# A two-layer graph attention kernel: where the first inputs of layer 2 lie, and when br1's product is made

## The chip, the cores and the metric

The kernel runs on one core of a Trainium2 chip. The metric is the time of the whole program on the device in microseconds (us), median of several runs. A core has five engines with a queue each: TensorE (PE in the profile; its weight loads are PEld), VectorE (DVE), ScalarE (ACT), GpSimd (POOL) and SyncE (SP). SP does no arithmetic here: it issues DMA transfers. POOL issues the indirect DMAs, which gather or scatter rows by a list of row numbers. Both kinds of transfer run on the core's 16 DMA engines. [...] an instruction that waits holds up everything behind it in its queue.

## The reference

There are 10000 nodes with 768 features and 170000 edges (80000 drawn, their reverses, and a loop at each node), sorted by target. Cut to what matters:

```python
def gat_conv(x, edge_index, W, a_src, a_dst, bias, heads, out_ch, concat):
    xl = (x @ W).reshape(n, heads, out_ch)
    e = leaky_relu(alpha_src[src] + alpha_dst[dst], 0.2)
    e = exp(e - segment_max(e, dst)[dst])
    alpha = e / (segment_sum(e, dst)[dst] + 1e-16)
    return segment_sum(xl[src] * alpha, dst) + bias

h1 = relu(layer_norm(gat_conv(x, W1, 4 heads of 256), g1, be1)) + (x @ Wr1 + br1)
h2 = layer_norm(gat_conv(h1, W2, 1 head of 768), g2, be2) + (h1 @ Wr2 + br2)
out = plain_layer_norm(x + h2)
```

All of it is float32. The kernel never adds br1 to h1: it carries h1 - br1. What br1 contributes behind it is a row that is the same for every node: br1 @ W2 for layer 2's attention, br1 @ Wr2 for its residual.

## The kernel before, in words

**Stages.** The first stage makes table 1 (x @ W1 and its attention logits for each node) and sorts the nodes by degree. Then 79 tiles of 128 nodes are worked through twice, by `ordered_layer1` and by `ordered_layer2`. A tile's nodes have about the same degree, so a tile is `SLOTS[t]` gathers of 128 table rows, one row for each node: 8, 10, 11, 12, 12, 13 slots for the first tiles, up to 41 in the middle, and down to 9 at the end. Layer 1 writes each tile's product h1 @ W2 to table 2 in DRAM (`table2`), its transposed h1 to `h1_d` and its x to `x_d`. Layer 2 gathers rows of all tiles from table 2, so its gathers begin once layer 1's last row of tiles has landed.

**Layer 2, for each tile t.** The first slot holds the tile's own rows and comes by SP (L452); the others are gathered by POOL (L424). VectorE makes the logits e from the last columns of the slots (L477 to L499). The 768 columns are then weighted and summed over the slots: the first 512 by VectorE into `acc` (`weigh`, L519), the last 256 by TensorE, which multiplies each slot with a diagonal matrix of its weights (diagonals by ScalarE at L891, products at L892, bias at L887). TensorE also makes the residual r = x + h1 @ Wr2 in PSUM (`residual`, L903 for x, L906 for h1). After the last slot VectorE takes the statistics of the sum (L561, in `norms`), normalises with g2 and be2, adds r, takes statistics again, and ScalarE and an indirect DMA of POOL (L925) write the rows out.

**Buffers.** The ring holds `RING2` = 38 slots of 770 floats a partition. Slot q of all tiles, counted through, lies at q modulo 38. `ring.fetch(upto)` issues the loads of all slots below `upto`; a gather into a used slot waits until VectorE and TensorE have read it. The ring belongs to pool `b2`, which lies where layer 1's pool `b1` lay: the first instruction that uses `b2` on an engine waits until all work on `b1` is done. `wr2` takes the place of `wr1`, outside these pools, and is loaded earlier. The transposed h1 and the x of a tile come by SP into `parts` (`fetch_x`, L867 and L868), pieces of the memory of W2, two for each kind in turn; `ins` holds those that are on their way.

**Constants.** `spread` loads a vector to all 128 partitions (L143). At the start of layer 2, b2, g2, be2, br2 and `shift` (br1 @ W2) are spread; `be2_b` gets br2 (L860), `b2_b` gets the shift (L861). br1 is copied along the free axis into `brT` (L585), and the product brT @ wr2 (L952, recorded at the helper's line L171) gives br1 @ Wr2 in all partitions; it is added to `be2_b` at L973, ahead of the first tile's statistics.

**Order.** Inside a stage the order is written out by hand: each engine executes its instructions in the order of the program. In tile t's loop over its slots, VectorE also makes the logits of tile t + 1 (at slot `turn`) and the norm of tile t - 1 (at slots 3, 6 and 9), between the sums. SP's order at the start of layer 2 is: Wr2; b2, g2, be2; br2, shift; the own row of tile 0; h and x of tile 0; h and x of tile 1; then own rows of tiles 1, 2, 3 inside the ring (`ring.fetch(RING2)`, L931). TensorE's order is residual(0); tile 0's weights; br1's product; residual(1); tile 1's weights; residual(2). GpSimd issues 7 gathers for tile 0 (L859) and then the 27 others that the ring holds, 34 in all, before slots are used again.

Of the kernel before, what the change touches and what calls it, by code (L numbers as in the profile page):

```python
# [35 lines left out]
P = 128  # L36
# [11 lines left out]
RING2 = 38  # L48
# [31 lines left out]
def gnn_kernel(ctx, tc, x, x_cols, src, dst, src_col, dst_col, W1, a_src1, a_dst1, b1, g1, be1, Wr1, br1,  # L80
               W2, a_src2, a_dst2, b2, g2, be2, Wr2, br2, out, n_edges):
    nc = tc.nc
    N, D0 = out.shape
# [6 lines left out]
    NT = -(-N // P)  # L90
# [48 lines left out]
    def spread(pool, v, name, queue=None):  # L139

        n = v.shape[-1] if len(v.shape) == 1 else v.shape[0] * v.shape[1]
        b = pool.tile([P, n], F32, name=name)
        (queue or nc.scalar).dma_start(b, bass.AP(tensor=v.tensor, offset=v.offset, ap=[[0, P], [1, n]]))  # L143
        return b
# [437 lines left out]
    def spread_br1(pool, name):  # L582

        to = pool.tile([P, K1, P], F32, name=name)
        nc.vector.tensor_copy(to, br1_c[:, :, None].to_broadcast([P, K1, P]))  # L585
        return to
# [259 lines left out]
    def ordered_layer2():  # L846
        nonlocal ps_big
        with tc.tile_pool(name="b2", bufs=1) as pool, tc.tile_pool(name="small2", bufs=2) as small, \
                tc.tile_pool(name="ps_acc2", bufs=2, space=PSUM) as ps_acc, \
                tc.tile_pool(name="ps_q2", bufs=3, space=PSUM) as ps_big, tc.manual_schedule():  # L850

            wr2 = wr1.rearrange("p k n -> p (k n)")[:, :K1 * C2].rearrange("p (k n) -> p k n", n=C2)
            load(wr2, Wr2)
            parts = pieces(w2.rearrange("p k n -> p (k n)")[:, :6 * C1], C1)
            b2_b, g2_b, be2_b = (spread(pool, v, n, nc.sync)
                                 for v, n in ((b2, "b2"), (g2, "g2"), (be2, "be2")))
            adds = [spread(pool, br2, "out", nc.sync), spread(pool, shift, "brT", nc.sync)]
            ring = Ring(pool, table2, R2, RING2, dict(zip(FIRST, TURNS)))
            ring.fetch(SLOTS[0])  # L859
            nc.vector.tensor_add(be2_b, be2_b, adds[0])  # L860
            nc.vector.tensor_add(b2_b, b2_b, adds[1][:, :C2])  # L861
            brT = spread_br1(pool, "brT")

            def fetch_x(t):

                hT, xt = parts[t % 2], parts[2 + t % 2][:, :D0]
                nc.sync.dma_start(hT, h1_d[t])  # L867
                nc.sync.dma_start(xt, x_d[t])  # L868
                return hT.rearrange("p (k n) -> p k n", n=P), xt

            ones = pool.tile([1, P], F32, name="ones")
            nc.vector.memset(ones, 1.0)

            def whole(t):
                return SLOTS[t] <= ring.size

            def weights_of(t):


                n = SLOTS[t]  # L880
                ad = small.tile([P, H2], F32, name="ad")
                nc.vector.tensor_add(ad, ring.slot(FIRST[t])[:, C2:C2 + H2], lift)
                e, _ = logits(small, ring, FIRST[t], FIRST[t] + n, ad, H2, C2)
                yield e
                normalised(small, e, H2, t)
                to = rs[t][:, C2:2 * C2 - ON_PE2]
                nc.tensor.matmul(to, ones, b2_b[0:1, ON_PE2:], start=False, stop=False, skip_group_check=True)  # L887
                for k in range(n):
                    if k % G == 0:
                        diagonals = pool.tile([P, G, P], F32, name="diagonals", bufs=DIAGONALS)  # L890
                    nc.scalar.activation(diagonals[:, k % G, :], ident, AF.Copy, scale=e[:, k, :])  # L891
                    nc.tensor.matmul(to, diagonals[:, k % G, :], ring.slot(FIRST[t] + k)[:, ON_PE2:C2],  # L892
                                     start=False, stop=(k == n - 1), skip_group_check=True)
                yield

            def residual(t):


                hT, xt = ins.pop(t)
                r = ps_big.tile([P, 2 * BANK], F32, name="big")  # L900
                for c in range(0, C2, BANK):
                    d = min(C2, c + BANK)
                    nc.tensor.matmul(r[:, c:d], ident, xt[:, c:d], start=True, stop=False,  # L903
                                     skip_group_check=True)
                    for j in range(K1):
                        nc.tensor.matmul(r[:, c:d], hT[:, j, :], wr2[:, j, c:d], start=False,  # L906
                                         stop=(j == K1 - 1 and (d < C2 or not whole(t))),
                                         skip_group_check=True)
                return r

            def norms(t, h, r, means):

                stats = deviation(small, [a for m in means for a in pieces(m, C2 - ON_PE2)])
                yield
                scaled(h, means, stats, g2_b, be2_b)
                nc.vector.tensor_add(h, h, r[:, :C2])
                mean, inv = deviation(small, pieces(h, C2 // 2))
                yield
                nc.vector.reciprocal(inv, inv)
                less = small.tile([P, 1], F32, name="less")  # L920
                nc.vector.scalar_tensor_tensor(less, mean, -1.0, inv, op0=OP.mult, op1=OP.mult)
                o = pool.tile([P, C2], F32, name="out")
                nc.scalar.activation(o, h, AF.Identity, bias=less, scale=inv)
                yield
                nc.gpsimd.indirect_dma_start(  # L925
                    out=out, out_offset=bass.IndirectOffsetOnAxis(ap=nodes(t), axis=0),
                    in_=o, in_offset=None, bounds_check=N - 1, oob_is_err=False)

            assert C2 % BANK and C2 % BANK + C2 - ON_PE2 <= BANK
            ins = {t: fetch_x(t) for t in range(min(2, NT))}  # L930
            ring.fetch(RING2)  # L931
            rs = {0: residual(0)}
            last = iter(())
            ready = []
            assert whole(0) and NT > 1
            for t in range(NT):
                n = SLOTS[t]
                if 0 < t < NT - 1:
                    rs[t + 1] = residual(t + 1)
                h = parts[4 + t % 2][:, :C2]  # L940
                if not whole(t):
                    for _ in last:
                        pass
                    ad = small.tile([P, H2], F32, name="ad")
                    nc.vector.tensor_add(ad, ring.slot(FIRST[t])[:, C2:C2 + H2], lift)
                    attend_parts(small, ring, h, h, ad, b2_b, H2, DH2, t)
                    last = norms(t, h, rs[t], [h])
                else:
                    e = (ready or list(weights_of(t)))[0]
                    acc = ps_acc.tile([P, BANK], F32, name="acc")  # L950
                    if not t:
                        q = product(brT, wr2, C2)  # L952
                        rs[1] = residual(1)
                    next(last, None)
                    ready, ahead, turn = [], iter(()), n
                    if t + 1 < NT and SLOTS[t + 1] + LEAD <= ring.size:

                        ahead = weights_of(t + 1)
                        turn = min(max(n // 3, n + SLOTS[t + 1] + 2 * LEAD - ring.size), n - LEAD)
                    for k in range(n):  # L960
                        if k in (turn, turn + LEAD):
                            ready += itertools.islice(ahead, 1)
                        if k in (LEAD, 2 * LEAD, 3 * LEAD):
                            next(last, None)
                        weigh(acc, ring.slot(FIRST[t] + k), e[:, k], ON_PE2, None if k else b2_b)
                        ring.fetch(FIRST[t] + k + 1 + ring.size)
                        if t + 2 < NT and k == n // 2:
                            ins[t + 2] = fetch_x(t + 2)
                    ready += ahead
                    for _ in last:  # L970
                        pass
                    if not t:
                        nc.vector.tensor_add(be2_b, be2_b, q[:, :C2])  # L973
                    last = norms(t, h, rs[t], [acc, rs[t][:, C2:2 * C2 - ON_PE2]])
                if t + 2 < NT and t + 2 not in ins:
                    ins[t + 2] = fetch_x(t + 2)
            for _ in last:
                pass
# [270 lines left out]
```

## Time and profile before

| What | us |
|---|---|
| median of 3 runs | 5388.15 (5386.93 to 5388.26) |
| the profiled execution | 5386.19 |
| its span, first to last instruction | 5384.3 |
| busy in the span: PE / DVE / ACT / POOL | 4721.3 / 4348.2 / 3138.9 / 3238.2 |
| layer 1's last row of table 2 issued by SP | 3433.48 |
| layer 2's first gather on POOL | 3437.43 |
| TensorE's first product of layer 2 | 3461.82 |
| last instruction, the last rows out on POOL | 5372.45 |

Times in the profile count from the start of the span. A row of the timeline is: start, length in us, engine, line and operation, output and inputs with partitions x elements, how many, and in brackets how long the engine stood idle before it and what released it. "SPq" and "POOLq" are the queues' own instructions. The tile names are cut at their first digit, so that `w` stands for W2's memory (parts) and `wr` for Wr1's (wr2), `big` for any of TensorE's results. A row of windows gives each engine's busy time in a stretch, then the granted clock of TensorE as a share of full speed, the busy share of the DMA engines and what they moved in GB/s. The slices of the page are fortieths of the span, 134.6 us each, with the busy share in tenths; layer 2 fills slices 25 to 39. The ends of products are modelled, so a busy TensorE isn't one at its peak.

### The profile page before, as it was taken

Reading aid. Unit: us, or ns where it says so; the run is one execution under the profiler, and the core shown is the slowest. Engines: PE = TensorE matmul, PEld = TensorE weight load, DVE = VectorE, ACT = ScalarE, POOL = GpSimd, SP = SyncE. Lnnn points to the kernel's source line nnn. Section 1 sums busy time; section 2 is a strip of 40 time slices with the busy share of each in tenths; the row PEclk is TensorE's granted clock in tenths of the full one; section 3 lists DMA queues with packets and bytes.
Section 4 is the critical chain, followed back from the end, with each engine's and each line's share of the span. In section 5 each row is a group of like instructions: output and inputs, shape, how many; then the busy total and the mean of one; then the engine's idle time right before and its main releaser. Section 6 shows DMA issues by size and latency. Waiting matters only on the chain. (4 is left out here: it accounts for less than half of the span.)

```text
span 5384.3 us, 59633 instructions
## 1 busy us (share of the span) xinstructions
PE 4721.3 (88%) x15011; PEld 2818.7 (52%) x15011; DVE 4348.2 (81%) x8008; ACT 3138.9 (58%) x8204; POOL 3238.2 (60%) x3159
## 2 busy tenths in 40 slices
PE   8999996999999886478999999799988846889998
PEld 3444443555555543245555555466665534556665
DVE  5784244899999888888999999499887876878998
ACT  3434343787888877778888888344433313334443
POOL 3446455455666665556666554367776766767774
PEclk9999998999999998789999999899998978989999
DMA  4333635899999996899999998699999998999995
GB/s 155 126 98 90 90 93 202 307 338 342 359 358 369 358 346 252 306 323 355 359 365 362 350 334 303 221 327 377 369 337 327 332 301 301 341 328 354 369 382 216
DMA packets 474308, 1591.37 MB, mean 296 GB/s; under 512 B 118327, under 2 KB 122487, under 8 KB 473958
## 3 DMA queue, kind: packets, MB, share of 16 engines
q0 software_dynamic: 322384, 1286.62, 66.3%
q1 hardware_dynamic: 149520, 297.43, 16.3%
q10 hardware_dynamic: 2054, 3.42, 0.2%
q8 instruction: 126, 2.06, 0.2%
q14 instruction: 224, 1.84, 0.1%
HBM read 1431.80 MB, written 177.29 MB: 299 GB/s over the span
## 5 line engine op out<-in xcount | busy, mean ns | idle before, releaser
L424 POOL DMA_INDIRECT ring<-table,slots x2675 | 2659.6, 994 | 1486.7 <-DVE acc L519 366.4
L519 DVE SCALAR_TENSOR_TENSOR acc<-ring,e,acc 128x256 f32<-128x256 f32 (+1 forms) x2538 | 1570.8, 619 | 113.3 <-PE acc L725 37.7
L508 ACT ACTIVATE ring<-ring,e 128x256 f32<-128x256 f32 x3320 | 1351.5, 507 | 0.2
L515 DVE TENSOR_TENSOR acc<-acc,ring 128x1024 f32<-128x1024 f32 x830 | 1021.3, 1230 | 80.6 <-ACT ring L508 9.2
L171 PE MATMUL big<-w,xT 128*128 128x512 f32 x1896 | 826.1, 597 | 27.0 <-DMA w<-in_W_dram 9.6
L906 PE MATMUL big<-wr,w 128*128 128x512 f32 (+1 forms) x2528 | 846.4, 488 | 0.0
L892 PE MATMUL big<-ring,diagonals 128*128 128x256 f32 x2672 | 667.2, 412 | 193.3 <-ACT diagonals L891 180.3
L171 PE MATMUL big<-wr,xT 128*128 128x512 f32 x1896 | 835.4, 597 | 0.2 <-ACT xT L688 0.2
L803 PE MATMUL half<-w,hT 128*128 128x512 f32 (+1 forms) x2528 | 830.4, 486 | 0.0
L892 PEld LDWEIGHTS big<-ring,diagonals 128*128 128x128 f32 x2672 | 548.2, 208 | 309.8 <-ACT diagonals L891 211.8
L803 PEld LDWEIGHTS half<-w,hT 128*128 128x128 f32 x2528 | 477.8, 189 | 372.7 <-issue 310.7
L906 PEld LDWEIGHTS big<-wr,w 128*128 128x128 f32 x2528 | 482.6, 191 | 340.1 <-issue 307.5
L725 PE MATMUL acc<-ring,diagonals 128*128 128x256 f32 x1816 | 452.2, 406 | 220.5 <-ACT diagonals L719 220.2
L171 PEld LDWEIGHTS big<-w,xT 128*128 128x128 f32 x1896 | 362.5, 192 | 486.5 <-issue 467.6
L171 PEld LDWEIGHTS big<-wr,xT 128*128 128x128 f32 x1896 | 357.7, 192 | 421.6 <-issue 420.9
L725 PEld LDWEIGHTS acc<-ring,diagonals 128*128 128x128 f32 x1816 | 365.9, 204 | 299.7 <-ACT diagonals L719 242.7
L891 ACT ACTIVATE diagonals<-ident,e 128x128 f32<-128x128 f32 x1336 | 400.5, 387 | 147.6 <-DVE e L499 129.3
L565 ACT ACTIVATE sd<-mv,eps 128x1 f32<-128x1 f32 x237 | 69.8, 295 | 638.0 <-DVE mv L563 637.7
L649 DVE TENSOR_TENSOR scr<-big,ad_b 128x1024 f32<-128x1024 f32 x79 | 96.7, 1224 | 381.6 <-ACT row L646 381.6
L654 POOL TENSOR_TENSOR row<-row,none 128x1024 f32<-128x1024 f32 x79 | 187.0, 2368 | 266.8 <-ACT row L646 266.3
L719 ACT ACTIVATE diagonals<-ident,e 128x128 f32<-128x128 f32 x908 | 278.5, 387 | 117.6 <-DVE e L499 117.6
L485 ACT ACT_TABLE_LOAD x153 | 196.3, 1283 | 219.7 <-DVE e L484 108.1
(172 smaller groups left out, 3813.4 us busy)
## 6 DMA issues: line engine op xcount, KB each, us to landing
ring<-table,slots POOLq DMA_INDIRECT x2675, 6.9
table<-row SPq DMA_DIRECT2D x79, 516.0 KB, 3.7
h_d<-hT SPq DMA_DIRECT2D x79, 512.0 KB, 6.9
w<-h_d SPq DMA_DIRECT2D x79, 512.0 KB, 8.3
table<-row SPq DMA_DIRECT2D x79, 385.0 KB, 6.4
ring<-table SPq DMA_DIRECT2D x79, 385.0 KB, 6.4
xT<-in_x_cols_dram SPq DMA_DIRECT2D x79, 384.0 KB, 4.5
x_d<-xt SPq DMA_DIRECT2D x79, 384.0 KB, 6.7
```

Of the source, the lines that this page charges most:

```text
L171: nc.tensor.matmul(p[:, c:e], aT[:, j, :], w[:, j, c:e], start=(j == 0), stop=(j == k - 1))
L424: nc.gpsimd.indirect_dma_start(out=to, out_offset=None, in_=table, in_offset=bass.IndirectOffsetOnAxis(ap=index, axis=0), **more)
L485: nc.scalar.activation(e, e, AF.Exp)
L508: nc.scalar.activation(row[:, s], row[:, s], AF.Copy, scale=e[:, h:h + 1])
L515: nc.vector.tensor_add(acc[:, :c], acc[:, :c], row[:, :c])
L519: nc.vector.scalar_tensor_tensor(acc[:, s], row[:, s], e[:, h:h + 1], (acc if first is None else first)[:, s], op0=OP.mult, op1=OP.add)
L719: nc.scalar.activation(diagonals[:, k * H1 + i, :], ident, AF.Copy, scale=e[:, k, i:i + 1])
L725: nc.tensor.matmul(acc[:, c:d], diagonals[:, k * H1 + i, :], ring.slot(FIRST[t] + k)[:, c:d], start=(k == 0 and c % BANK == 0), stop=(k == ...
L803: nc.tensor.matmul(q, hT[:, j, :], w2[:, j, c:c + q.shape[1]], start=(j == 0), stop=(j == K1 - 1))
L891: nc.scalar.activation(diagonals[:, k % G, :], ident, AF.Copy, scale=e[:, k, :])
L892: nc.tensor.matmul(to, diagonals[:, k % G, :], ring.slot(FIRST[t] + k)[:, ON_PE2:C2], start=False, stop=(k == n - 1), skip_group_check=True)
L906: nc.tensor.matmul(r[:, c:d], hT[:, j, :], wr2[:, j, c:d], start=False, stop=(j == K1 - 1 and (d < C2 or not whole(t))), skip_group_check= ...
```

## The change

Layer 2's first inputs leave W2's memory. The ring is made first, and its last 4608 floats a partition (slots 32 to 37, all but 12 floats of them) hold, from the end downwards: the spread br1 (1024), h and x of tile 1 (1024 and 768), h and x of tile 0. Later tiles use `parts` as before. With that:

- br1 is spread into the ring's end as VectorE's first instruction of the stage, and its product is TensorE's first, ahead of residual(0).
- SP's order becomes: Wr2; h and x of tile 0; own row of tile 0; shift; b2; h and x of tile 1; g2, be2; br2; own rows of tiles 1 to 3.
- `ring.fetch(RING2)` moves behind residual(1), since slots 32 to 37 are free only then.
- br2 is added to be2 at the end of tile 0's loop, just ahead of br1 @ Wr2, in place of the start; br2 and the shift share a buffer with `out`, so `brT` as a tile of the pool is gone.

```diff
-            b2_b, g2_b, be2_b = (spread(pool, v, n, nc.sync)
-                                 for v, n in ((b2, "b2"), (g2, "g2"), (be2, "be2")))
-            adds = [spread(pool, br2, "out", nc.sync), spread(pool, shift, "brT", nc.sync)]
             ring = Ring(pool, table2, R2, RING2, dict(zip(FIRST, TURNS)))
-            ring.fetch(SLOTS[0])
-            nc.vector.tensor_add(be2_b, be2_b, adds[0])
-            nc.vector.tensor_add(b2_b, b2_b, adds[1][:, :C2])
-            brT = spread_br1(pool, "brT")
+            rest, flat = RING2 * R2, ring.rows.rearrange("p k n -> p (k n)")
+
+            def at_end(n):
+                nonlocal rest
+                rest -= n
+                return flat[:, rest:rest + n]
+
+            brT = at_end(C1).rearrange("p (k n) -> p k n", n=P)
+            nc.vector.tensor_copy(brT, br1_c[:, :, None].to_broadcast([P, K1, P]))
+            firsts = [(at_end(C1), at_end(D0)) for _ in range(min(2, NT))][::-1]
 
             def fetch_x(t):
 
-                hT, xt = parts[t % 2], parts[2 + t % 2][:, :D0]
+                hT, xt = firsts[t] if t < 2 else (parts[t % 2], parts[2 + t % 2][:, :D0])
...
+            ins = {0: fetch_x(0)}
+            ring.fetch(SLOTS[0])
+            adds = [spread(pool, shift, "out", nc.sync)]
+            b2_b = spread(pool, b2, "b2", nc.sync)
+            ins[1] = fetch_x(1)
+            g2_b, be2_b = (spread(pool, v, n, nc.sync) for v, n in ((g2, "g2"), (be2, "be2")))
+            nc.vector.tensor_add(b2_b, b2_b, adds[0][:, :C2])
+            adds.append(spread(pool, br2, "out", nc.sync))
+            assert SLOTS[0] <= rest // R2 and NT > 1
...
-            ins = {t: fetch_x(t) for t in range(min(2, NT))}
-            ring.fetch(RING2)
+            q = product(brT, wr2, C2)
             rs = {0: residual(0)}
...
                     if not t:
-                        q = product(brT, wr2, C2)
                         rs[1] = residual(1)
+                        ring.fetch(RING2)
...
                     if not t:
+                        nc.vector.tensor_add(be2_b, be2_b, adds[1])
                         nc.vector.tensor_add(be2_b, be2_b, q[:, :C2])
```

More of the change, by code (lines that the diff above doesn't have):

```diff
@@ L934, in ordered_layer2 @@
             ready = []
-            assert whole(0) and NT > 1
+            assert whole(0)
             for t in range(NT):
```

## The prediction

> **What bounds the kernel now.** I read the slices of the page first, then the windows of 20 us around the change of layers, then the timeline there, then VectorE's waits behind it.
>
> ```profile
> span 5384.3 us, 59633 instructions
> ...
> PE   8999996999999886478999999799988846889998
> ...
> DVE  5784244899999888888999999499887876878998
> ...
> DMA  4333635899999996899999998699999998999995
> ```
>
> One notch matters here: at slice 25 the table for layer 2 has just been completed, and DVE falls to 4 and DMA to 6. The windows resolve it (columns: length, busy us of PE, weight load, DVE, ACT, POOL, then clock, DMA share, GB/s):
>
> ```profile
> 3420.00:3440.00 20.00, 12.98 (x46) 7.63 (x44) 0.00 (x0) 2.51 (x5) 1.95 (x3) 0.93 0.30 105
> 3440.00:3460.00 20.00, 0.00 (x0) 0.00 (x0) 2.90 (x5) 0.00 (x0) 11.88 (x12) 0.50 1.02 293
> 3460.00:3480.00 20.00, 18.18 (x51) 10.60 (x52) 7.66 (x26) 5.00 (x14) 12.11 (x13) 0.80 1.02 402
> 3480.00:3500.00 20.00, 20.00 (x61) 11.21 (x60) 9.69 (x21) 6.54 (x13) 13.76 (x15) 1.00 1.01 394
> 3520.00:3540.00 20.00, 20.00 (x74) 13.55 (x73) 18.44 (x40) 9.06 (x24) 12.14 (x13) 1.00 0.87 303
> ```
>
> Up to 3500 the DMA engines are full, while TensorE first has nothing and then cannot stop; at 3520 to 3540 TensorE and VectorE are full and the DMA engines are not (0.87). The timeline says why (start, us, engine, line):
>
> ```profile
> 3433.48 0.32 SPq L747 DMA_DIRECT2D table<-row  x1
> 3436.61 0.33 SPq L143 DMA_DIRECT2D b<-in_b_dram  x1
> 3440.22 0.89 SPq L868 DMA_DIRECT2D w<-x_d  x1
> 3460.21 0.17 DVE L477 TENSOR_TENSOR e<-ring,ad 128x8 f32<-128x8 f32 x1 [5.27 <-DMA ring<-table,slots]
> 3461.82 2.05 PE L903 MATMUL big<-w,ident 128*128 128x512 f32 x2 [28.78 <-DMA w<-x_d]
> 3475.19 0.17 DVE L477 TENSOR_TENSOR e<-ring,ad 128x10 f32<-128x10 f32 x1 [3.57 <-DMA ring<-table,slots]
> 3480.78 10.48 PE L171 MATMUL big<-wr,brT 128*128 128x512 f32 x32
> 3484.23 0.95 POOL L424 DMA_INDIRECT ring<-table,slots  x1 [0.30 <-issue]
> 3491.30 0.95 DVE L973 TENSOR_TENSOR be<-be,big 128x768 f32<-128x768 f32 x1 [9.93 <-PE big L171]
> 3502.80 0.69 PE L887 MATMUL big<-b,ones 1*128 1x256 f32 x2
> 3504.39 0.94 POOL L424 DMA_INDIRECT ring<-table,slots  x1 [5.71 <-DVE sd L919]
> ```
>
> TensorE waits 28.8 us for x of tile 0, which stands behind five spread vectors and an own row on SP's queue. It then does residual(0), tile 0's weights and br1's product in a row, and VectorE, through with tile 0's rows, stands 9.93 us for that product. Tile 1's slots come free late, and GpSimd's gathers stand 5.7 us (3498.7 to 3504.4). The delay is felt for a while after, as five tiles show in VectorE's waits, of 3508 to 3560 and of 3560 to 3620 (total us, times, longest):
>
> ```profile
> DVE st L561 <- PE big L892: 1.5, 2, 0.8
> DVE st L561 <- PE big L892: 1.7, 3, 0.8
> ```
>
> From 3740 on VectorE waits for gathers instead (4.3 us in 3740 to 3800, 4.6 in the next 60 us), and gathers for slots.
>
> **What the Trainium skill says.** "TensorE: Matmul & The Clock Gate", Part 1, What's actually happening: the throttled clock is the default, a window of some 3.4 us without work brings it back, and as much work releases it. The trace agrees: the last product ends at 3433.04, the clock is 0.78 in 3436 to 3438 and 0.50 until about 3467, some 5 us after TensorE begins. "DMA: Bandwidth & Descriptors", Queues, rings and completion order: each DMA engine takes packets in turn from the queues that have work. So SP's loads and GpSimd's gathers share the 16 engines, and order counts within a queue; the trace agrees, since x of tile 0 needs 21.6 us behind 2.3 MB of SP's own. "Perfetto Trace Analysis", Identifying the Most-Contended Engine: busy time of matmuls is no good measure of load; I use the period of a tile instead.
>
> **The change part by part.**
>
> Loads. SP's first load of this pool is released at 3436.61 by the last row's store; the new tiles lie in the same pool, so I let h and x of tile 0 start then and not earlier. What SP moved: two issues (0.49 and 0.89 us) go ahead of five spreads (about 0.4 us each) and the own row; h and x of tile 1 ahead of g2, be2 and br2. The bytes ahead of tile 1's own row stay 4.1 MB, so its landing (3471.5) stays. By the record of before, 1152 KB of SP's queue had landed at 3442.5, so x of tile 0 (896 KB) is there by about 3442. In before x of tile 1 landed at 3468.8; it now has 1.2 MB less ahead of it. A new wait: br2 goes into the shift's buffer, so SP stands until VectorE has added shift and b2 (2049 KB of the queue, so about 3452), and the own rows of tiles 1 to 3 stand behind it. I cost it at nothing, because SP's transfers already issued keep the engines busy to about 3465; without that cover tile 1's logits are late one for one.
>
> TensorE. The spread of br1 (0.69 us on VectorE) no longer waits for the sums of L860 and L861, so the product starts at about 3437.5; Wr2 was issued at 3410.96 and took about 10 us. It takes 10.48 us, plus the throttled start: in before the first two groups of residual(0) took 2.05 and 9.12 us against 1.02 and 7.03 of residual(2), 3.1 us more. It ends near 3451. residual(0), 11.7 us (3507.85 to 3519.55 for residual(2)), to 3462.7. Weights of tile 0 wait for the logits, whose gathers I leave at 3460.2, and diagonals at 3463.6; 4.2 us (3476.59 to 3480.78), to 3468. residual(1) to 3479.6, in place of 3502.8. Then tile 1's diagonals (3479.15 on) and 5.1 us: 3485 in place of 3507.85. residual(2) needs h and x loaded at about 3478, which took 9.6 us: start 3490, and with a throttled start of 2.6 its weights end near 3510, in place of 3525. TensorE is **15 us** ahead.
>
> VectorE. Tile 1's logits wait for the same gathers (3475.19), so tile 0's rows are done at 3481.4 as before. The 9.93 us go; the sum with br2, moved here, costs 0.95: **9.0 us** ahead. Next it wants tile 2's last gather, issued at 3477.98 and 8.5 us under way, so 3486.5, at 3495.80 - 9.0 = 3486.8: just in time. h and x of tile 3, whose buffers are now free at once, come some 20 us earlier and put 0.9 MB (2.4 us at 380 GB/s) in the way; I charge 0.5. The waits of five tiles for TensorE, 1.5 + 1.7 = **3.2 us**, go too, as TensorE leads by more.
>
> Gathers. Slots 32 to 37 now hold the first inputs, so the gathers into them wait for the product, residual(0) and residual(1), and GpSimd's queue waits behind them, with every later gather and the first store of rows out. The first that needs residual(1) is slot 34, the 31st gather, at 3484.23 in before. residual(1) ends at 3479.6: hidden by 4.6 us; without that cover it costs its delay one for one. The stalls at 3498.7, 3515.7 (4.5 us), 3534 and later go, since tiles 1 to 4 free their slots earlier; at 1.25 us a gather the queue can gain more than 12 us before 3620.
>
> Sum: 9.93 - 0.95 + 3.2 - 0.5 = **11.7 us**. After 3740 gathers, VectorE and slots wait for each other in a ring, nothing is tied to absolute time, and I let the lead pass unchanged to the end. The profiled execution took 5386.19 (span 5384.3 and 1.9 around it), so 5374.5; the median of the runs is 1.96 above it: **5376.4**.
>
> Bounds not shown in the trace: tile 0's gathers may land 3 us earlier or later, since the spreads now share time with later gathers (-3 to +3); the lead in the stage of gathers is kept between a third and, if TensorE's lead decides, the whole of 15 to 17.
>
> **Rivals.** *Partly given back* (0.20): the DMA engines, 0.87 to 0.96 busy between 3500 and 3640, have only 12.4 us of idle share, and the extra early loads and queueing eat some of it. For it: share 1.00 from 3640. Against: they moved 402 GB/s at 3460, and 370 there. Gain 3 to 9: 5379 to 5385. *TensorE's lead decides* (0.12): if gathers run 15 us ahead by 3600, VectorE's later waits for them shrink too; 5370 to 5373. *Nothing arrives* (0.06): tile 1 and 2 are limited by the full DMA engines whatever TensorE does, 5386 to 5390; against it stands the 9.93 us wait that names the product. *Slower* (0.06): gathers stand for residual(1). It decides from an end after 3484 plus the 12 us gained, so 3496; if tile 1's inputs or tile 0's logits come so late that residual(1) ends where it did, 3502.8, GpSimd stands 18.6 us and the net is +7: 5395. Against: x of tile 1 now has less ahead of it.
>
> **How the numbers follow.** My forecast, gain 10 to 14, has 0.56. The measurement can tell about 0.2% from no change, 10.8 us. Of the forecast 0.48 lies beyond that, and TensorE's 0.12: faster 0.60. The rest of the forecast, given back and nothing: about 0.33 same. Slower 0.07. The range 5370 to 5385 takes gains of 3 to 18 and leaves out the last two rivals and little more.
>
> **What would show it.** br1's product starts near 3437.5 and ends near 3451; residual(0) follows without a gap; VectorE's 9.93 us wait is gone; residual(1) ends before the gather of slot 34; the gathers no longer stand at 3498.7; the waits of L561 for TensorE are gone up to 3620, and the wait of VectorE for gathers begins about 12 us sooner. Wrong it would be if gathers wait on L906 or L171 after 3484, if the loads of h and x do not land before 3451, or if the lead at 3600 is there and the end has not moved.

## The result, and the profile after

The changed kernel takes 5374.60 us (median of 8 runs, 5369.76 to 5378.14), the kernel before beside it 5388.98 (8 runs, 5386.93 to 5391.94). The ratio is 0.9971, 95% interval 0.9961 to 0.9982: 14.4 us or 0.27% less, and 1.8 us below the forecast of 5376.4. The profiled execution of the changed kernel took 5377.65, with a span of 5375.9.

The two spans differ by only 8.4 us, because layer 1, whose code is the same in both, ended later in the second execution: SP issued its last row of table 2 at 3435.89 and not at 3433.48. So all comparisons of traces here count from that row. From there to the end it is 1950.8 us before (5384.31 - 3433.48) and 1940.0 after: 10.9 us less.

The page of the changed kernel, slices of 134.4 us:

```profile
span 5375.9 us, 59639 instructions
...
PE   8999996999999886478999999999988846889998
...
DVE  5884244899999888888999999599887786778998
```

At slice 25 PE has risen from 7 to 9 and DVE from 4 to 5. The windows of 20 us of the changed kernel show more (busy us of PE, weight load, DVE, ACT, POOL, then clock, DMA share, GB/s):

```profile
3440.00:3460.00 20.00, 19.96 (x51) 10.31 (x52) 1.10 (x3) 0.00 (x0) 12.31 (x13) 0.91 1.00 280
3480.00:3500.00 20.00, 17.17 (x57) 10.81 (x56) 17.54 (x42) 9.22 (x22) 14.75 (x15) 0.91 1.02 402
3520.00:3540.00 20.00, 20.00 (x74) 13.44 (x72) 18.50 (x41) 7.90 (x18) 15.35 (x16) 1.00 1.00 381
```

TensorE, which had nothing to do in 3440 to 3460, is full. VectorE's busy time in 3480 to 3500 went from 9.69 to 17.54. And at 3520 to 3540 GpSimd issues 16 instructions in place of 13, so that the DMA engines are full (1.00, before 0.87). The timeline of the changed kernel from layer 1's last row on (start, us, engine, line, idle time before and its releaser):

```profile
3435.89 0.32 SPq L747 DMA_DIRECT2D table<-row  x1
3440.04 12.28 PE L171 MATMUL big<-wr,ring 128*128 128x512 f32 x32 [4.59 <-DVE ring L865]
3452.16 1.02 PE L917 MATMUL big<-ring,ident 128*128 128x512 f32 x2
3463.19 0.17 DVE L477 TENSOR_TENSOR e<-ring,ad 128x8 f32<-128x8 f32 x1 [6.49 <-DMA ring<-table,slots]
3467.03 5.41 PE L906 MATMUL big<-ring,diagonals 128*128 128x256 f32 x16 [2.48 <-ACT diagonals L905]
3472.28 1.02 PE L917 MATMUL big<-ring,ident 128*128 128x512 f32 x2
3476.87 0.17 DVE L477 TENSOR_TENSOR e<-ring,ad 128x10 f32<-128x10 f32 x1 [2.83 <-DMA ring<-table,slots]
3484.01 0.95 DVE L987 TENSOR_TENSOR be<-be,big 128x768 f32<-128x768 f32 x1
3486.28 1.37 POOL L424 DMA_INDIRECT ring<-table,slots  x1 [0.30 <-PE big L906]
3490.01 0.17 DVE L477 TENSOR_TENSOR e<-ring,ad 128x11 f32<-128x11 f32 x1 [1.53 <-DMA ring<-table,slots]
```

The product runs while the loads land, and residual(0) (L917 at 3452.16) follows it without a gap. The sum with br1's product (L987) waits for nothing: the 9.93 us are gone. The gather of slot 34 (3486.28) comes after residual(1), which ended at 3483.98, and stands only its usual 0.30. What is left of VectorE's waits from 3480 to 3620 (total us, times, longest):

```profile
DVE e L477 <- DMA ring<-table,slots: 1.5, 1, 1.5
DVE sd L576 <- ACT sd L565: 0.7, 1, 0.7
```

VectorE no longer waits for TensorE at all. In the kernel before this list was 9.9 us for br1's product and 3.2 us of L561.

**Where the lead goes.** A lead here is how much earlier than in the kernel before the same step comes. The table follows one gather (the 101st of layer 2) and two additions of residuals on VectorE (those of tiles 8 and 20), each counted from layer 1's last row in its own trace. First the two rows of before, then those of after, for the gather and for tile 20:

```profile
3597.82 0.94 POOL L424 DMA_INDIRECT ring<-table,slots  x1 [0.30 <-issue]
3889.06 0.95 DVE L916 TENSOR_TENSOR w<-w,big 128x768 f32<-128x768 f32 x1
```

```profile
3583.55 0.95 POOL L424 DMA_INDIRECT ring<-table,slots  x1 [0.30 <-DVE acc L519]
3875.12 0.95 DVE L930 TENSOR_TENSOR w<-w,big 128x768 f32<-128x768 f32 x1
```

The gather: 3597.82 - 3433.48 = 164.34 against 3583.55 - 3435.89 = 147.66, a lead of 16.7. Tile 20: 455.58 against 439.23, a lead of 16.3. In the same way for the kernels of the experiments below:

| kernel | gather 101 | VectorE, tile 8 | VectorE, tile 20 | end of the span |
|---|---|---|---|---|
| product first, loads as before | 10.5 | 10.5 | 12.7 | 11.8 |
| loads first, product as before | 11.3 | 6.6 | 13.5 | 15.4 |
| the change | 16.7 | 11.1 | 16.3 | 10.9 |
| the change, another execution | 17.4 | 12.0 | 20.9 | 16.1 |
| the change, late vectors | 15.8 | 11.0 | 17.6 | 17.3 |
| order alone, two executions | 18.0, 17.8 | 12.1, 13.1 | 19.3, 17.9 | 15.1, 14.9 |
| order alone, both loads first | 18.2 | 13.4 | 22.0 | 19.0 |
| the same, waits by tile | 19.9 | 15.2 | 22.2 | 17.5 |

At tile 20, where VectorE waits for gathers, it is about as far ahead as the gathers were at 3600, and up to 4 us more. The kernel with the loads alone shows it best: VectorE's 6.6 us become 13.5. The waits show both steps, each time first before, then after. From 3480 to 3620 GpSimd stands less for TensorE's products (L892, in the changed kernel L906), which free its slots; from 3740 to 3900 VectorE stands less for gathers:

```profile
POOL ring L424 <- PE big L892: 19.8, 23, 4.5
POOL ring L424 <- PE big L906: 6.9, 19, 1.4
DVE e L477 <- DMA ring<-table,slots: 13.5, 6, 2.6
DVE e L477 <- DMA ring<-table,slots: 7.3, 3, 2.5
```

No kernel moves the gathers alone, so that their lead decides rests on these waits and on the order of the rows of the table. To the end up to 5.4 us of that are lost, in all but one (loads first); the last column is one execution each against the one trace of before, and two executions of the changed kernel differ by 5.2 there.

### The profile page after: what moved, and what is told of

It reads as the page before. It is cut to its first block, busy times and chain, and to the rows that moved or that the text cites. A ratio compares the mean times of both kernels' runs of the same rounds, so it can differ in the third digit from the quotient of the medians.

```text
span 5375.9 us, 59639 instructions
## 1 busy us (share of the span) xinstructions
PE 4731.0 (88%) x15011; PEld 2826.0 (53%) x15011; DVE 4347.3 (81%) x8008; ACT 3137.8 (58%) x8204; POOL 3242.5 (60%) x3159
## 3 DMA queue, kind: packets, MB, share of 16 engines
q1 hardware_dynamic: 149520, 297.43, 16.3%
## 5 line engine op out<-in xcount | busy, mean ns | idle before, releaser
L906 PE MATMUL big<-ring,diagonals 128*128 128x256 f32 x2672 | 675.4, 416 | 193.2 <-ACT diagonals L905 185.4
L920 PE MATMUL big<-wr,w 128*128 128x512 f32 (+1 forms) x2464 | 823.2, 487 | 0.0
L906 PEld LDWEIGHTS big<-ring,diagonals 128*128 128x128 f32 x2672 | 553.7, 210 | 312.4 <-ACT diagonals L905 211.7
L920 PEld LDWEIGHTS big<-wr,w 128*128 128x128 f32 x2464 | 469.8, 191 | 330.4 <-issue 298.6
```

## The experiments

The runs of the experiments fall into three sets, on three chips, each beside its own runs of the kernel before: 5385.03 us in the first (30 runs), 5648.39 in the second (51) and 5391.76 in the third (9). Ratios are taken within a set. My theory was that either half of the change, the product first or the loads first, already takes VectorE's wait away, so that the halves don't add; the rivals were that they add, that the gathers held up by the new place take part of the gain, and that the place of the first inputs, not the order, is what counts.

### Product first, loads as before

```diff
+            brT = pool.tile([P, K1, P], F32, name="brS")
+            nc.vector.tensor_copy(brT, br1_c[:, :, None].to_broadcast([P, K1, P]))
             nc.vector.tensor_add(be2_b, be2_b, adds[0])
-            brT = spread_br1(pool, "brT")
...
+            q = product(brT, wr2, C2)
             rs = {0: residual(0)}
...
-                        q = product(brT, wr2, C2)
                         rs[1] = residual(1)
```

> Only br1's product is moved to the front of TensorE's work; the loads of h and x keep their place behind the five vectors, in W2's memory. Theory A (what counts is VectorE's 9.9 us wait for the product; either half of the change removes it): the wait at the sum of be2 and the product is gone, TensorE is some 10.5 us ahead from residual(1) on, VectorE 9 us at the first tile's norm, and the time is 9 to 11 us below the kernel before, most of the change's 14. Theory B (what counts is how much of TensorE's idle time is filled, and the two halves add up): the product fills 10.5 of about 23 us, so the gain is about 6 us.

Measured: 5374.80 us (22 runs), ratio 0.9984 (0.9978 to 0.9990), 8.6 us below before by the ratio (0.0016 of 5385). The timeline of this kernel:

```profile
3435.03 13.07 PE L171 MATMUL big<-wr,brS 128*128 128x512 f32 x32 [4.34 <-DVE brS L861]
3460.62 2.07 PE L904 MATMUL big<-w,ident 128*128 128x512 f32 x2 [12.52 <-DMA w<-x_d]
3477.53 0.95 DVE L974 TENSOR_TENSOR be<-be,big 128x768 f32<-128x768 f32 x1
```

and one row of its waits of VectorE from 3480 to 3620:

```profile
DVE st L561 <- PE big L893: 3.7, 6, 0.8
```

The product fills time in which TensorE waited for x anyway, and VectorE's wait (L974) is gone. But TensorE then stands 12.5 us for x. It ends residual(1) at 3490.0, 58.9 us after layer 1's last row (in before 69.3, in the changed kernel 48.1), and goes on level with VectorE: the waits of L561 stay, 3.7 us of them. The gathers are 10.5 us ahead and VectorE 10.5: nothing more is gained later, other than 2 us by tile 20. The interval of the ratio (5.4 to 11.8 us) holds both what my theory expected and the 6 us of the other; it is the trace that speaks for mine.

### Loads first, product as before

```diff
-            q = product(brT, wr2, C2)
             rs = {0: residual(0)}
...
                     if not t:
+                        q = product(brT, wr2, C2)
                         rs[1] = residual(1)
```

> Only the loads are moved: h and x of the first two tiles lie at the ring's end and come first, but the product stays between tile 0's weights and residual(1). Theory A: the product ends near 3479 to 3482 us, when VectorE wants it, so its wait shrinks to at most 1 us; residual(1) ends near 3491 to 3494 instead of 3484, so the gathers for slots 34 to 37 stand 5 to 8 us behind it; net gain 8 to 11 us. Theory B: 12.6 of 23 us filled, gain about 7.5 us, and the sum of this gain and of the product's alone is that of the change. Rival of my prediction (gathers that stand for residual(1) decide): gain 4 us or less.

Measured: 5374.43 us (8 runs), ratio 0.9978 (0.9968 to 0.9988), 11.8 us below before. Its timeline:

```profile
3469.45 10.48 PE L171 MATMUL big<-wr,ring 128*128 128x512 f32 x32
3481.19 0.95 DVE L987 TENSOR_TENSOR be<-be,big 128x768 f32<-128x768 f32 x1
3490.09 0.94 POOL L424 DMA_INDIRECT ring<-table,slots  x1 [5.25 <-PE big L920]
```

The product ends at 3479.9, before VectorE wants it at 3481.2: this half alone takes the wait away too. Whether the gains of the halves add, the times can't tell. By the ratios the halves give 8.6 and 11.8 us, together 20.4, and the whole 15.6 in its first measurement (9.7 to 21.0) and 19.4 in the third set. The traces do tell: 9.93 us are taken away once, and at tile 8 VectorE's leads of 10.5 and 6.6 would add to 17.1, where the whole change has 11.1 and 12.0. What the whole has over either half is the gathers' lead, 16.7 and 17.4 against 10.5 and 11.3.

Here the gathers do stand for residual(1), 5.25 us, which ends at 3491.5: the mechanism of the prediction's slower rival is real. VectorE pays later, when its lead falls to 4.5 at tile 3: it stands for ScalarE, and ScalarE had stood until earlier rows were stored by GpSimd's queue:

```profile
3535.96 1.03 ACT L937 ACTIVATE out<-w,less,sd 128x768 f32<-128x768 f32 x1 [9.70 <-DMA out_dram<-out,order]
3542.14 0.16 DVE L576 RECIPROCAL sd<-sd 128x1 f32<-128x1 f32 x1 [4.52 <-ACT sd L565]
```

The time is below before all the same.

### The order alone

The order of the change, with the first inputs where they were, in W2's memory, so that the ring's last slots are free and `ring.fetch(RING2)` needn't wait for residual(1).

```diff
...
-            brT = at_end(C1).rearrange("p (k n) -> p k n", n=P)
-            nc.vector.tensor_copy(brT, br1_c[:, :, None].to_broadcast([P, K1, P]))
-            firsts = [(at_end(C1), at_end(D0)) for _ in range(min(2, NT))][::-1]
+            brT = spread_br1(pool, "brT")
...
-                hT, xt = firsts[t] if t < 2 else (parts[t % 2], parts[2 + t % 2][:, :D0])
+                hT, xt = parts[t % 2], parts[2 + t % 2][:, :D0]
...
             adds.append(spread(pool, br2, "out", nc.sync))
...
+            ring.fetch(RING2)
...
                         rs[1] = residual(1)
-                        ring.fetch(RING2)
```

> The order of loads and products is the change's, but nothing lies at the ring's end: h and x of the first two tiles stay in W2's memory, br1's spread in a tile of its own, and the ring is filled without waiting for residual(1). Theory A: memory plays no part, time as the changed kernel within 3 us (a gain of 12 to 17 us over before), TensorE's products within 1 us of the changed kernel's relative to layer 1's last row. Rival (the place is what brings it, because W2's pieces are then free for tiles 2 and 3 at once): residual(2) starts later than 8 us after tile 1's weights, and a third or more of the gain is lost.

> The changed order with the first inputs in W2's memory. Theory 1, the place is no part of the gain and costs some: their load moves into the idle time of the DMA engines before layer 1's last row has landed, so tile 1's logits start 2 to 4 us sooner after that row than in the changed kernel, and the time is 2 to 6 us below the changed kernel beside it. Theory 2, the end of the ring is what the gain rests on: no better than before, 12 us or more above the changed kernel. Theory 3, the last measurement of it was chance: within 2 us of the changed kernel.

Measured in the first set: 5371.25 us (5 runs), ratio 0.9964 (0.9951 to 0.9977). In the third: 5374.32 (5 runs), ratio 0.9962 (0.9949 to 0.9976), beside the changed kernel:

> The changed kernel again, as the mark for the three kernels beside it. Every theory: 10 to 16 us below before (5373 to 5379 where before takes 5389). If it is less than 7 or more than 19 below, the difference between sets of runs is as large as what the other kernels are to tell, and they are to be read against this one alone.

which took 5371.29 (5 runs), ratio 0.9964 (0.9951 to 0.9978). That is 20.5 us below its before and not the 14.4 of the first measurement, more than the 19 that I had set as a limit; so the third set is read against this run. The order alone is then 3.0 us above the changed kernel by medians, and the means of five are 5371.9 for both. The place at the end of the ring is no part of the gain. The theory that it costs 2 to 6 us of the whole time is not borne out either, though the trace has its mechanism (this is the third set):

```profile
3433.90 0.32 SPq L862 DMA_DIRECT2D w<-h_d  x1
3434.77 0.32 SPq L863 DMA_DIRECT2D w<-x_d  x1
3437.35 0.32 SPq L747 DMA_DIRECT2D table<-row  x1
```

In W2's memory the loads of h and x go out 3.5 us ahead of layer 1's last row, in time that the DMA engines had free (their share was 0.00 from 3430 to 3434); at the ring's end they go out 3.3 us behind it (3439.22 after 3435.89). Tile 1's logits start 38.3 us after that row (3475.67 - 3437.35; in the first set 38.2) and 41.0 and 40.0 in two executions of the changed kernel. VectorE's lead at tile 0 is 12.3 instead of 8.2 and 9.2. At tile 3 the leads are already 11.0 and 9.8 in this set: VectorE stands 2.98 us for ScalarE there, and 1.00 in the changed kernel. At tile 8 the difference between the two kernels is 2 us at most, and the gathers lead by 17.8 and 17.4: the same. From 3740 on (about tile 12) VectorE goes by the gathers, so what is left of it does not arrive either.

### Vectors that are wanted late go last

```diff
             ins[1] = fetch_x(1)
-            g2_b, be2_b = (spread(pool, v, n, nc.sync) for v, n in ((g2, "g2"), (be2, "be2")))
             nc.vector.tensor_add(b2_b, b2_b, adds[0][:, :C2])
-            adds.append(spread(pool, br2, "out", nc.sync))
...
                         ring.fetch(RING2)
+                        g2_b, be2_b = (spread(pool, v, n, nc.sync) for v, n in ((g2, "g2"), (be2, "be2")))
+                        adds.append(spread(pool, br2, "out", nc.sync))
```

> As the changed kernel, but g2, be2 and br2 (1152 KB) are loaded behind the own rows of tiles 1 to 3. Theory A: up to tile 1's logits the full DMA engines set VectorE's time, so these logits come 3 to 4 us sooner (near 3473 instead of 3476.9), VectorE's lead at the first norm rises from 9.7 to 12 or 13 us, and the time is 2 to 4 us below the changed kernel's. Rival (the bytes come back as a later wait): tile 2's logits wait longer for their gathers than the 1.5 us of the changed kernel and the time is the changed kernel's within noise.

Measured: 5364.84 us (5 runs), ratio 0.9960 (0.9947 to 0.9973), but not for the reason given. Tile 1's own row came sooner, and VectorE then waited longer for the gathers: 9.0 us ahead of tile 1's logits in place of 2.83. The logits start 40.4 us after layer 1's last row, against 41.0 and 40.0 in the changed kernel. In this one trace, moving loads behind others inside SP's queue didn't hasten the gathers in GpSimd's, in keeping with what the Trainium skill ("DMA: Bandwidth & Descriptors", Queues, rings and completion order) says on engines that take the queues in turn. With leads of 15.8 (gathers) and 17.3 (end) near those of the changed kernel (16.7 and 17.4, 10.9 and 16.1), I take the low time for the spread between executions; that was not settled.

### The second set: a chip on which layer 2 takes 14% longer

> The kernel before, unchanged, profiled once more, to see how much VectorE's times of each tile differ between two executions of one kernel when counted from layer 1's last row. Theory: within 0.5 us up to tile 12 (about 3700 us), where every program shows the same steps, and some 5 us apart in the stage where gathers and slots wait for each other (3740 to 5000 us). Rival (the stage adds nothing of its own, and the 5 to 6 us that the changed kernels gain in it are an effect of the change): within 1 us there too.

> The changed kernel, unchanged, timed on the chip of the two kernels below and profiled once more. Theory: 10 to 16 us below before; VectorE's first norm 8 to 8.5 us ahead as in the first profile, and an end 11 to 16 us ahead, since only the later stage differs between executions.

> As the kernel with the order alone (nothing at the ring's end), but h and x of tile 1 are also loaded at once, behind those of tile 0 and ahead of layer 2's other loads: 896 KB more go through in the idle 6 us of the DMA engines around layer 1's last row. Theory (the bytes that SP and GpSimd have to move between the first gather and tile 1's logits set those logits; their order within SP's queue does not): logits of tile 1 come 36 us after the issue of layer 1's last row, against 38.2 in the kernel with the order alone and 41.0 in the changed one; first norm 14 to 15 us ahead of before, and a gain of 17 to 22 us. Rival (gathers have a rate of their own): 38 us, and the time of the order alone.

> As the kernel above, but a tile of layer 2's pool waits only for the tiles of layer 1 whose memory it takes, not for the whole pool: own row, shift and vectors start right behind layer 1's last row instead of 3 us later, and br1's product follows layer 1's last product without the 4.4 us pause and the throttled start. Theory of the bytes: logits of tile 1 some 33 to 34 us after the issue of layer 1's last row, gain 2 to 3 us more than the kernel above (19 to 25 us below before). Rival (TensorE's start counts, not the bytes): br1's product ends 6 us sooner but tile 1's logits stay at 36 us and the time is that of the kernel above.

Measured: before again 5652.53; the changed kernel 5643.77 (14 runs), ratio 0.9984 (0.9972 to 0.9997); both loads first 5644.46 (22), ratio 0.9988 (0.9977 to 0.9999); waits by tile 5644.44 (22), ratio 0.9986 (0.9978 to 0.9995). The changed kernel is faster here too, by 0.03 to 0.28%: 9.0 us by the ratio, where 10 to 16 were expected, and 11.4 by the traces from layer 1's last row on. The three kernels can't be told apart. From layer 1's last row to the end the kernel before takes 2214.9 us here and not 1950.8; its VectorE is 8.9 us behind the first trace of that kernel at tile 0 and 58 at tile 20. So this chip has no answer to how far two executions of it differ on the others. That row itself goes out at 3435.88 here, and at 3449.29, 3446.35 and 3438.90 in the three kernels beside it.

The early stage can be read all the same: tile 1's logits start 39.0 us after that row with both loads first, where 36 was expected and 38 by the rival, and 35.9 us with waits by tile, where 33 to 34 was expected. TensorE's waits in layer 2 of the kernel before, on this chip:

```profile
PE big L892 <- issue: 130.0, 84, 23.0
PE big L906 <- issue: 120.0, 103, 3.1
```

"Issue" is time in which the profile shows nothing that it waited for; the first trace of before has none of it. But there TensorE stands for ScalarE's diagonals instead, of which 47.1 us are left on this chip:

```profile
PE big L892 <- ACT diagonals L891: 180.3, 38, 23.0
```

So the 250 us are not all added. From layer 1's last row to the end TensorE's idle time goes from 301 to 447 us and its busy time from 1650 to 1768: 145 and 119 of the 264 us. In the fourth kernel single products of residual(1) stand up to 2.9 us each, and VectorE's first statistics then 18.3 us for them. What held TensorE up was not shown, so the two kernels were run again in the third set.

### Both loads first, and waits by tile

Both on top of the order alone; the second has the second diff as well.

```diff
-            ins = {0: fetch_x(0)}
+            ins = {t: fetch_x(t) for t in range(2)}
...
-            ins[1] = fetch_x(1)
```

```diff
-        with tc.tile_pool(name="b2", bufs=1) as pool, tc.tile_pool(name="small2", bufs=2) as small, \
+        with tc.tile_pool(name="b2", bufs=1, reuse_waits="tile") as pool, tc.tile_pool(name="small2", bufs=2) as small, \
```

> As the order alone, with h and x of tiles 0 and 1 both issued ahead of the other loads of the stage. Theory 1 (bytes ahead of tile 1's logits are the bound at 3440 to 3490): 1.8 MB in place of 0.9 MB move into idle DMA time, so tile 1's logits start another 1 to 3 us sooner and the time is 0 to 3 us below the order alone. Rival, VectorE's lead is set by then by tile 2's gathers, which need the same bytes: the same as the order alone within 2 us.

> As the kernel with both loads first, with the pool of the ring told to wait for the old tiles of its own memory and not for all of layer 1's pool. If what keeps the first spreads and the own row until after layer 1's last row is the wait for the whole old pool, the spreads start before 3433 and the time is another 1 to 4 us lower. Rival, the spreads overlap layer 1's last tiles' memory, so nothing starts sooner: the same within 1 us.

Measured: 5365.89 us (5363.26 to 5372.50, 5 runs), ratio 0.9955 (0.9941 to 0.9969), and 5368.98 (5367.23 to 5373.05), ratio 0.9959 (0.9946 to 0.9973). Both loads first is 5.4 us below the changed kernel of the set by medians, with one of its five runs inside the other's range (5370.40 to 5373.79); it was the fastest kernel of this set, but the intervals of the two ratios overlap, so "better than the change" is possible and not shown. Against the order alone it is 8.4 lower, where 0 to 3 were expected; the traces give 4.1 at the end and 0.4 in the gathers' lead. Nor did the theory's step come: tile 1's logits start 39.2 us after layer 1's last row (38.3 with the order alone), later and not 1 to 3 us sooner. The loads ahead are not free here. That row, with h of tile 1 ahead of it as well, lands 5.6 us after its issue and not 2.9, and GpSimd's first gather starts 6.6 us after the issue and not 3.9 (5.5 and 6.4 us with waits by tile). So what makes this kernel's time low is not shown, and it may be spread.

Waits by tile did start the stage's loads earlier: the product follows 0.03 us after the last row's issue, at 3433.84, and the own row goes out 1.1 us behind it and not 5.8. Tile 1's logits start 36.8 us after that row and not 39.2, VectorE's lead rises by 1.9 at tile 0 and 1.8 at tile 8, the gathers' by 1.7; the end does not follow (17.5, was 19.0), nor does the median (3.1 us higher). The expected 1 to 4 us were seen in the early stage only.

## Why the prediction was right, step by step

**VectorE: right to a microsecond, and so was the sum behind it.** Tile 1's logits were to start as in before: 41.0 us after layer 1's last row, in before 41.7, so 0.7 sooner. 9.93 - 0.95 + 0.73 = 9.7, and the first statistics come 9.7 ahead (forecast 9.0). Tile 2's gathers, called just in time with 0.5 us to pay, cost 1.53: 8.2 left. The waits of L561 gave back their 3.2: 11.4, and VectorE is 11.1 ahead at tile 8 (forecast 11.7).

**TensorE: right, with three terms mis-sized.** All times here less the 2.41 us by which layer 1 ended later. The product started at 3437.6 (forecast 3437.5). Its throttled start cost 1.8 (12.28 - 10.48), not 3.1. residual(0) ended at 3461.5 (3462.7), residual(1) at 3481.6 (3479.6): tile 0's weights took 5.4 and not 4.2 and began a microsecond later. The throttled start of residual(2) cost 1.6, not 2.6. TensorE was 16.7 ahead after tile 2's weights (forecast 15).

**Gathers behind residual(1): right, with half the cover.** 2.3 us of it were left (3486.28 - 3483.98), not 4.6. The kernel with the loads alone shows what happens without: 5.25 us of standing. (The stall that the prediction puts at 3515.7 began at 3516.7, when the gather issued at 3515.7 was done.)

**The loads: right.** In the kernel with the loads alone residual(0) could start at 3441.7, with the last row at the same time as in before; the forecast had x of tile 0 there by about 3442. SP did stand for the shift's buffer (br2 goes out at 3456.58, right behind VectorE's sum), and it cost nothing: what ended the wait for tile 1's logits was gathers.

**After 3740: the step that was wrong, though the number held.** "I let the lead pass unchanged to the end." It did not pass unchanged: VectorE's 11 us became 16.3 and 20.9 at tile 20 in the two traces of the changed kernel. From 3740 on VectorE waits for gathers, so the gathers' lead of about 17, which goes with TensorE's (16.7), counts and not VectorE's own. That is the mechanism of the rival "TensorE's lead decides", to which I gave 0.12. Towards the end 5 us are lost again (10.9 and 16.1), as in "partly given back" (whose DMA share of 0.87 to 0.96 between 3500 and 3640 should begin at 0.77; its 12.4 us of idle share include that). The two sets put the whole gain at 14.4 and 20.5 us: the first inside the forecast's 10 to 14 but for 0.4, the second beyond the rival's 18. So that the forecast was within 2 us of its first measurement is in part luck: the lead taken from the wrong engine happened to lie near what is left at the end. Where the late loss comes from was not found: it differs by 5 us between two executions of one kernel.

**Slower, or nothing.** Neither occurred; the slower rival decides from an end of residual(1) near 3496 on, and it ended at 3484.

## What to carry to other kernels

Where two engines hand buffers on in a ring, follow the lead of each of them, gathers too, up to the stage in which one begins to wait for the other: the lead that counts there is that of the engine that is waited for. Work that depends on nothing from the stage, such as br1's product, can fill the pause before the first inputs. Inputs loaded into memory that is free before the old stage ends can go out early, but here no time was shown to come of it, and with a second pair of loads ahead the old stage's last row landed 2.7 us later. Two ways of removing one wait remove it once. A gain of 0.3% is measured against layers that vary by more: compare traces from a common event just ahead of the change.

## What the runs showed of the hardware

- Layer 1, with the same code, issued its last row anywhere from 3429.38 to 3437.35 us in the ten profiled executions outside the second set, 8 us apart. Two executions of the changed kernel differ by 5.2 us behind that row as well. Both may have a part in the 3 to 21 us by which the runs of one changed kernel differ in the first and third sets.
- br1's product takes 10.48 us in the middle of work and 10.59 after a pause of 0.47. After pauses of 4.34 to 4.59 it takes 12.04 to 13.19, after 7.23 and 7.29 it takes 13.55 and 13.02. In the changed kernel the granted clock was still 1.00 in 3436 to 3440, while TensorE stood, and 0.58 and 0.56 in the next two windows of 2 us, when it had begun to work. The Trainium skill ("TensorE: Matmul & The Clock Gate", Part 1, What's actually happening) speaks of a window of about 3.4 us that runs free of the program's start, so the drop need not come with the pause; that this is the reason here is not shown.
- On one chip layer 2 of the kernel before took 2214.9 us and not 1950.8, with TensorE busy 119 us longer and idle 145 us longer; 250 us of its waits there have no cause that the profile names. Layer 1's last row went out at 3435.88 in that kernel, as on the other chips, but at 3438.90 to 3449.29 in the three beside it. The cause stays open.
